# One more 512 KB transfer in a load queue: sample 0 loaded a second time, into a slot that is still empty

## The chip, the core and the metric

The kernel runs on one core of one Trainium2 chip. The core has a matrix engine (TensorE, "PE" in the profile), a vector engine (VectorE, "DVE"), three further engines that are used here for issuing and waiting alone (ScalarE "ACT", GpSimd "POOL", SyncE "SP"), and 16 DMA engines that move data between the memory outside the core (HBM, "DRAM" in the code) and its own memory (SBUF, 128 partitions). The metric is the time of one execution in microseconds (us). The kernel before takes 323.55 us, the median of three runs (323.35, 323.55 and 323.56).

## The reference

There are 128 samples, each a matrix x[b] of 128 channels by 1024 points in 32-bit floats (512 KB). Each sample has a subject number between 0 and 7, which chooses one of eight 128 by 128 weight matrices:

```
w = weights[subjects]                       # 128 x (128, 128)
out = x + einsum('bct,bcd->bdt', x, w)      # out[b] = x[b] + w[b]^T x[b]
```

So 64 MB (67.1 million bytes) are read, as many are written, and each sample needs one 128 by 128 by 1024 product and one addition.

## The kernel before

**Tiles and slots.** The samples go in turns of four (`G * H` = 2 * 2), so there are `NT` = 32 turns. SBUF holds `x_all`, which is cut into `SLOTS` = 12 slots; a slot has room for the four samples of a turn, 16 KB in each of the 128 partitions. Turn i uses slot i % 12. The result is added into the slot in place and is stored from there, so a slot is free for the next load when its store has landed.

**Loads (ACT's queue).** ScalarE issues 128 transfers, one for each sample, in order (lines 206 to 210). `load` writes a sample as 128 partitions by 4 KB, and reads it as 32 pieces of 16 KB, which is what the rearrangement with `ROWS` = 4 says: one piece in DRAM is four rows of the sample, which go to four partitions. From turn 12 on, ScalarE waits ahead of the four loads of a turn until the store of the turn that had this slot has landed. The semaphore of a slot, `s_slot[k]`, is raised by 16 for each of the four loads and for the store. Sample 0 and 1 raise `s_head`, so that the first product can start early.

**Products (PE).** Per half turn (two samples), TensorE waits for `s_go` (the weights stand ready) and `s_ready` (the data has landed; GpSimd turns the landing of loads into it, lines 212 to 217), and does four products of 128 by 128 by 512 into a half of PSUM.

**Additions (DVE).** Per half turn, VectorE waits for the products and adds them to the slot in one operation of 128 by 2048 (line 180), then copies the weights of two samples of the next turn into their place (line 159).

**Stores (SP's queue).** SyncE waits for additions (`s_added`) and issues the stores. For the first 20 turns there is one store of 2 MB per turn, which waits for the additions of its own turn and of four more (`BEHIND`); the last 12 turns go in pairs (4 MB each). In a store of one turn each partition is read in one run of 16 KB and written to DRAM in four pieces of 4 KB. The last store is issued outside of the first critical block, behind waits that the end of the program needs.

**Order.** Nothing plans this order but the program itself: each engine runs its own list, and ACT's and SP's transfers are worked off by the same 16 DMA engines, each queue in its order.

Of the kernel before, what the change touches and what calls it, by code (L numbers as in the profile page):

```python
# [30 lines left out]
G = 2  # L31
H = 2
# [3 lines left out]
SLOTS = 12  # L36
# [9 lines left out]
DMA = 16  # L46
# [3 lines left out]
ROWS = 4  # L50
# [5 lines left out]
def transfer(nc, engine, out, in_):  # L56

    later, nc._always_lower_symbolic_ap = nc._always_lower_symbolic_ap, False  # L60
    ins, outs = engine.lower_ap_dma(in_), engine.lower_ap_dma(out)
    nc._always_lower_symbolic_ap = later
    return engine.add_instruction(
        mybir.InstDMACopy(
            name=nc.get_next_instruction_name(),
            engine=engine.engine,
            ins=ins,
            outs=outs,
            mode="Copy",
            cce_op=ALU.bypass,  # L70
            queue=QUEUES[engine.engine],
        )
    )


@with_exitstack
def kernel(
    ctx: ExitStack,
    tc: tile.TileContext,
    x: bass.AP,  # L80
    subjects: bass.AP,
    weights: bass.AP,
    out: bass.AP,
):
    nc = tc.nc
    B, C, T = x.shape
    S, _, D = weights.shape
    NT = B // (G * H)

    def sbuf(name, *shape, dtype=F32):  # L90
        return ctx.enter_context(nc.sbuf_tensor(name, list(shape), dtype)).ap()


    room = -(nc.sbuf_base + -nc.sbuf_base % 32) % ALIGN
    if room:
        sbuf("room", C, room // 4)
    x_all = sbuf("x_all", C, SLOTS * H * G * T)
    xs = [
        x_all[:, i * H * G * T : (i + 1) * H * G * T].rearrange("c (q t) -> c q t", t=T)
        for i in range(SLOTS)  # L100
    ]
    w_all = sbuf("w_all", C, S, D)
    ws = [sbuf(f"w{i}", C, 1, D) for i in range(H * G)]
    zeros = sbuf("zeros", C, N)
    given, near, wrap = (sbuf(name, 1, B, dtype=I32) for name in ("given", "near", "wrap"))
    index = sbuf("index", 1, B + H * G, dtype=I32)
    ps = [
        ctx.enter_context(nc.psum_tensor(f"ps{i}", [D, G, T], F32)).ap() for i in range(P_SLOTS)
    ]

    s_given = tc.alloc_semaphore("s_given")
    s_wall = tc.alloc_semaphore("s_wall")
    s_index = tc.alloc_semaphore("s_index")
    s_zeros = tc.alloc_semaphore("s_zeros")
    s_product = tc.alloc_semaphore("s_product")
    s_added = tc.alloc_semaphore("s_added")

    s_ready = tc.alloc_semaphore("s_ready")
    s_go = tc.alloc_semaphore("s_go")

    s_slot = [tc.alloc_semaphore(f"s_slot{k}") for k in range(SLOTS)]
    s_head = tc.alloc_semaphore("s_head")

    def emptied(i):
        turns = i // SLOTS
        return DMA * (H * G + 1) * turns - (DMA * G if i >= SLOTS and i % SLOTS == 0 else 0)

    def load(engine, i, q):
        transfer(
            nc,  # L130
            engine,
            xs[i % SLOTS][:, q, :],
            x[i * H * G + q].rearrange("(a r) t -> a (r t)", r=ROWS),
        ).then_inc(s_head if i * H * G + q < G else s_slot[i % SLOTS], DMA)

    def store(i, n):
        at = i % SLOTS * H * G * T
        return transfer(
            nc,
            nc.sync,  # L140
            out[i * H * G : (i + n) * H * G].rearrange("g d t -> d g t"),
            x_all[:, at : at + n * H * G * T].rearrange(
                "d (o t) -> d o t", o=1 if i >= NT - WHOLE else n
            ),
        )

    def subjects_of(i):
        _, subject = nc.values_load_multi_w_load_instructions(
            index[0:1, i] if isinstance(i, slice) else index[0:1, bass.ds(i * (H * G), H * G)],
            engines=[mybir.EngineType.DVE],  # L150
            min_val=0,
            max_val=S - 1,
            skip_runtime_bounds_check_because="the index is clamped on the chip above",
        )
        return subject

    def place(h, subject):
        for q in range(h * G, (h + 1) * G):
            copy = nc.vector.tensor_copy(ws[q], w_all[:, bass.ds(subject[q], 1), :])  # L159
        copy.then_inc(s_go, 1)  # L160

    def multiply(slot, h):
        nc.tensor.wait_ge(s_go, 1).then_inc(s_go, -1)
        nc.tensor.wait_ge(s_ready, 1).then_inc(s_ready, -1)  # L164
        for q in range(h * G, (h + 1) * G):
            for t in range(0, T, N):
                at = slot * (H * G * T) + (q * T + t)
                mm = nc.tensor.matmul(  # L168
                    ps[h][:, q % G, t : t + N],
                    ws[q][:, 0, :],  # L170
                    x_all[:, bass.ds(at, N)],
                    start=True,
                    stop=True,
                )
        mm.then_inc(s_product, 1)

    def add(slot, h):
        mine = x_all[:, bass.ds(slot * (H * G * T) + h * G * T, G * T)]
        nc.vector.wait_ge(s_product, 1).then_inc(s_product, -1)  # L179
        nc.vector.tensor_tensor(  # L180
            mine, ps[h].rearrange("d g t -> d (g t)"), mine, ALU.add
        ).then_inc(s_added, 1)

    with tc.tile_critical():  # L184

        nc.sync.dma_start(given, subjects.rearrange("(o b) -> o b", o=1)).then_inc(s_given, DMA)
        nc.sync.dma_start(w_all, weights.rearrange("s c d -> c s d")).then_inc(s_wall, DMA)

        nc.vector.memset(zeros, 0.0).then_inc(s_zeros, 1)  # L189
        nc.tensor.wait_ge(s_zeros, 1)  # L190
        for _ in range(IDLE):
            nc.tensor.matmul(  # L192
                ps[P_SLOTS - 1][:, G - 1, :N], zeros[:, :D], zeros, start=True, stop=True
            )

        nc.vector.memset(index[:, B:], 0).then_inc(s_index, 1)  # L199
        nc.vector.wait_ge(s_given, DMA)  # L200
        nc.vector.tensor_scalar(near, given, -S, S - 1, ALU.max, ALU.min).then_inc(s_index, 1)  # L201
        nc.vector.wait_ge(s_index, 2)
        nc.vector.tensor_scalar(wrap, near, 0, S, ALU.is_lt, ALU.mult).then_inc(s_index, 1)  # L203
        nc.vector.wait_ge(s_index, 3)
        nc.vector.tensor_tensor(index[:, :B], near, wrap, ALU.add).then_inc(s_index, 1)  # L205
        for i in range(NT):
            if i >= SLOTS:
                nc.scalar.wait_ge(s_slot[i % SLOTS], emptied(i))
            for q in range(H * G):
                load(nc.scalar, i, q)  # L210

        for i in range(NT):
            if i == 0:
                nc.gpsimd.wait_ge(s_head, DMA * G).then_inc(s_ready, 1)
                nc.gpsimd.wait_ge(s_slot[0], DMA * G).then_inc(s_ready, 1)
            else:
                nc.gpsimd.wait_ge(s_slot[i % SLOTS], emptied(i) + DMA * H * G).then_inc(s_ready, H)

        for i in [*range(NT - SLOTS), *range(NT - SLOTS, NT, PAIR)]:
            n = 1 if i < NT - SLOTS else PAIR  # L220
            nc.sync.wait_ge(s_added, (i + n + (BEHIND if i < NT - LAST else 0)) * H)
            if i + n < NT:
                store(i, n).then_inc(s_slot[i % SLOTS], DMA)


        nc.vector.wait_ge(s_index, 4)
        nc.vector.wait_ge(s_wall, DMA)
        subject = subjects_of(slice(0, H * G))
        for h in range(H):
            place(h, subject)  # L230
        with nc.vector.Fori(0, NT) as turn:  # L231
            subject = subjects_of(turn + 1)
            for h in range(H):
                add(turn % SLOTS, h)
                place(h, subject)
        with nc.tensor.Fori(0, NT) as turn:
            for h in range(H):
                multiply(turn % SLOTS, h)

    with tc.tile_critical() as waits:  # L240
        for i in range(NT - SLOTS, NT - PAIR, PAIR):
            nc.scalar.wait_ge(s_slot[i % SLOTS], emptied(i + SLOTS))
    last = store(NT - PAIR, PAIR)

    tc.add_manual_dep(
        last.ins,
        waits.name,
        mybir.DependencyInfo(mybir.DependencyClass.NoSync, mybir.DependencyReason.SCHED_ONLY),
        reason="the end of the program waits for it",
    )  # L250
# [27 lines left out]
```

## Time and profile before

| what | value |
|---|---|
| time, median of three runs | 323.55 us (323.35 to 323.56) |
| profiled execution, span from the first to the last instruction | 322.2 us |
| PE busy | 246.3 us, 76% of the span |
| DVE busy | 165.7 us, 51% |
| bytes moved by DMA | 134.76 MB, 418 GB/s on average |

The profile is of one execution. The page gives its span and no other time of its own; the median is 1.35 us longer than that span, which is what lies around the first and last instruction (and the difference between one execution and another). Two parts of the page are used below beside the totals: the share of time in which the 16 DMA engines had a packet under way, in 40 equal slices of the span (about 8 us each, in tenths, 9 is 90% or more), and the DMA queues, of which q10 is the one that ScalarE issues on (its 67.12 MB are the loads) and q1 is that of SyncE (the stores and the weights).

### The profile page before, as it was taken

The page shows a single profiled execution, that of the slowest core. Times are in us where ns is not written, and L with a number is a line of the kernel's source. Part 1 is how long each engine was busy: PE and PEld are TensorE (multiplying, and loading weights), DVE is VectorE, ACT ScalarE, POOL GpSimd, SP SyncE. Part 2 cuts the span into 40 slices and gives each one's busy share as a digit, 9 for nine tenths or more (in the row PEclk, how much of TensorE's full clock was granted, in tenths as well). Part 3 has the DMA queues.
Part 4 walks back from the last instruction along what each step waited for, and adds up shares of the span by engine and source line. Part 5 has one row for each costly group of instructions (what it writes and reads, how often), then busy time and mean ns, then how long its engine had stood idle before and what let it go on. Part 6 is the DMA issues. An engine that isn't in the chain of part 4 may idle for free. (4 is left out here: it accounts for less than half of the span.)

```text
span 322.2 us, 2368 instructions
## 1 busy us (share of the span) xinstructions
PE 246.3 (76%) x518; PEld 101.8 (32%) x518; DVE 165.7 (51%) x202; POOL 0.2 (0%) x4
## 2 busy tenths in 40 slices
PE   6999999999996974975987489885699994972000
PEld 2344444444442421331333134332244431430000
DVE  2276776777677345354355344762657666254000
POOL 0000000000000000000000000000000000000000
PEclk9799999999999797797899899997999998698555
DMA  7999999999999999999999999999999999999996
GB/s 271 425 429 429 425 423 401 429 425 423 425 423 427 430 431 429 423 425 423 427 421 429 429 433 427 423 425 423 427 423 429 429 431 427 427 435 433 419 427 264
DMA packets 11315, 134.76 MB, mean 418 GB/s; under 512 B 2481, under 2 KB 3506, under 8 KB 3506
## 3 DMA queue, kind: packets, MB, share of 16 engines
q10 hardware_dynamic: 6144, 67.12, 49.6%
q1 hardware_dynamic: 5170, 67.64, 49.5%
q14 instruction: 1, 0.01, 0.0%
HBM read 67.63 MB, written 67.11 MB: 418 GB/s over the span
## 5 line engine op out<-in xcount | busy, mean ns | idle before, releaser
L168 PE MATMUL ps<-x_all,w 128*128 x512 | 241.3, 629 | 44.1 <-PEq L164 38.4
L180 DVE TENSOR_TENSOR x_all<-ps,x_all 128x2048 f32 x64 | 146.7, 2292 | 122.7 <-DVEq L179 122.7
L168 PEld LDWEIGHTS ps<-x_all,w 128*128 128x128 f32 x512 | 100.0, 201 | 185.7 <-issue 185.2
L159 DVE COPY w<-w_all 128x128 f32 x132 | 23.2, 219 | 4.7 <-DMA w_all<-in_L_cond_weights_dram 4.7
L192 PE MATMUL ps<-zeros 128*128 128x512 f32 x6 | 4.9, 988 | 1.7 <-DVE zeros L189 1.7
L192 PEld LDWEIGHTS ps<-zeros 128*128 128x128 f32 x6 | 1.8, 328 | 3.7 <-issue 2.1
L189 DVE MEMSET zeros<- 128x512 f32 x1 | 0.5, 485 | 1.0 <-SPq L184 1.0
L201 DVE TENSOR_SCALAR near<-given 1x128 int32<-1x128 int32 x1 | 0.2, 214 | 0.6 <-DMA given<-in_itok_B_dram 0.6
L205 DVE CUSTOM_DVE_ANT_0 index<-near,wrap 1x256 uint16<-1x256 uint16 x1 | 0.3, 280 | 0.0
L203 DVE TENSOR_SCALAR wrap<-near 1x128 int32<-1x128 int32 x1 | 0.2, 215 | 0.0
L265 POOL MEMSET const-bfloat16-1.0<- 128x1 bf16 x1 | 0.1, 102 | 0.0
L265 POOL MEMSET const-uint8-127<- 128x1 uint8 x1 | 0.1, 102 | 0.0
L265 POOL MEMSET const-float32-0.0<- 128x1 f32 x1 | 0.1, 99 | 0.2 <-issue 0.2
L265 POOL MEMSET const-float32-1.0<- 128x1 f32 x1 | 0.1, 99 | 0.0
L265 DVE BASE_LOAD x1 | 0.0, 21 | 0.1
L199 DVE MEMSET index<- 1x4 int32 x1 | 0.1, 62 | 0.0
## 6 DMA issues: line engine op xcount, KB each, us to landing
x_all<-in_x_dram ACTq DMA_DIRECT2D x128, 512.0 KB, 30.7
out_dram<-x_all SPq DMA_DIRECT2D x20, 2048.0 KB, 17.0
out_dram<-x_all SPq DMA_DIRECT2D x6, 4096.0 KB, 30.5
w_all<-in_L_cond_weights_dram SPq DMA_DIRECT2D x1, 512.0 KB, 5.5
given<-in_itok_B_dram SPq DMA_DIRECT2D x1, 0.5 KB
```

Source lines behind the costliest of these rows:

```text
L159: copy = nc.vector.tensor_copy(ws[q], w_all[:, bass.ds(subject[q], 1), :])
L168: mm = nc.tensor.matmul(ps[h][:, q % G, t : t + N], ws[q][:, 0, :], x_all[:, bass.ds(at, N)], start=True, stop=True,)
L180: nc.vector.tensor_tensor(mine, ps[h].rearrange("d g t -> d (g t)"), mine, ALU.add).then_inc(s_added, 1)
L189: nc.vector.memset(zeros, 0.0).then_inc(s_zeros, 1)
L192: nc.tensor.matmul(ps[P_SLOTS - 1][:, G - 1, :N], zeros[:, :D], zeros, start=True, stop=True)
L199: nc.vector.memset(index[:, B:], 0).then_inc(s_index, 1)
L201: nc.vector.tensor_scalar(near, given, -S, S - 1, ALU.max, ALU.min).then_inc(s_index, 1)
L203: nc.vector.tensor_scalar(wrap, near, 0, S, ALU.is_lt, ALU.mult).then_inc(s_index, 1)
L205: nc.vector.tensor_tensor(index[:, :B], near, wrap, ALU.add).then_inc(s_index, 1)
L265: nc = _bacc.Bacc("TRN2", target_bir_lowering=False, num_devices=1)
```

## The change

Behind the four loads of turn 5 (the sixth slot), ScalarE issues one more transfer. It reads sample 0 again, in the same 32 pieces of 16 KB as its first load did, and writes each piece whole into one partition: partitions 0, 4, 8, up to 124, at the place in `x_all` where slot 11 begins (the twelfth slot; four samples of 4 KB each fill it, so 16 KB is the slot's whole room in a partition). It raises a new semaphore, `s_twice`. Ahead of the loads of turn 11, which are the first to fill this slot, ScalarE waits until the transfer has landed. No engine reads what it wrote, and turn 11's loads write over it.

```diff
     s_slot = [tc.alloc_semaphore(f"s_slot{k}") for k in range(SLOTS)]
+    s_twice = tc.alloc_semaphore("s_twice")
     s_head = tc.alloc_semaphore("s_head")
...
+    def twice(engine):
+        at = (SLOTS - 1) * H * G * T
+        transfer(
+            nc,
+            engine,
+            x_all[::ROWS, at : at + ROWS * T],
+            x[0].rearrange("(a r) t -> a (r t)", r=ROWS),
+        ).then_inc(s_twice, DMA)
...
         for i in range(NT):
             if i >= SLOTS:
                 nc.scalar.wait_ge(s_slot[i % SLOTS], emptied(i))
+            if i == SLOTS - 1:
+                nc.scalar.wait_ge(s_twice, DMA)
             for q in range(H * G):
                 load(nc.scalar, i, q)
+            if i == 5:
+                twice(nc.scalar)
```

## The prediction

> **What bounds the kernel now.** I read the slices of the span first, then the DMA queues, then the waits, and last the stretches one by one. These are rows of the page:
>
> ```profile
> span 322.2 us, 2368 instructions
> PE 246.3 (76%) x518; PEld 101.8 (32%) x518; DVE 165.7 (51%) x202; POOL 0.2 (0%) x4
> ...
> DMA  7999999999999999999999999999999999999996
> ...
> q10 hardware_dynamic: 6144, 67.12, 49.6%
> q1 hardware_dynamic: 5170, 67.64, 49.5%
> ```
>
> No compute engine is near full, but the DMA row has a 9 in 38 of 40 slices, and the two queues' packets together took 99.1% of what 16 engines have in the span. PE and DVE wait for data; the DMA engines wait for nobody. That is an average, so it has to hold in each stretch. In this view of stretches the columns are the stretch and its length, the busy time of PE, PEld, DVE and POOL, the granted TensorE clock, the DMA share and GB/s:
>
> ```profile
> 0.00:8.00 8.00, 4.93 (x6) 1.85 (x6) 1.57 (x9) 0.20 (x4) 1.00 0.75 266
> 8.00:48.00 40.00, 39.24 (x85) 16.41 (x86) 25.28 (x31) 0.00 (x0) 0.96 1.01 427
> 48.00:56.00 8.00, 8.00 (x20) 3.33 (x18) 5.74 (x9) 0.00 (x0) 1.00 0.99 395
> 62.00:165.00 103.00, 85.19 (x179) 35.30 (x178) 57.08 (x69) 0.00 (x0) 0.92 1.01 426
> 232.00:246.00 14.00, 13.32 (x31) 5.87 (x32) 7.97 (x11) 0.00 (x0) 1.00 1.00 424
> 284.00:322.20 38.20, 7.13 (x16) 2.96 (x16) 7.12 (x9) 0.00 (x0) 0.66 0.93 396
> ```
>
> From 8 us on, the share is 0.99 to 1.01 in every stretch but the last, whatever is moved: loads alone (8 to 48), loads and stores together (62 to 165), and also from 232 to 246, where the stores had run dry. The queues of that last stretch:
>
> ```profile
> q10 hardware_dynamic: 526, 5.82, 98.2%
> q1 hardware_dynamic: 23, 0.11, 2.0%
> ```
>
> The loads that were queued filled the engines there by themselves. When one queue is empty the other covers, so the end is set by the sum of all bytes. The end of the program says the same. This is SyncE's view of its waits:
>
> ```profile
> SPq L274 <- DMA out_dram<-x_all: 25.5, 1, 25.5
> ```
>
> The last store (4 MB) is out for 25.5 us. Alone at 427 GB/s its 4.19 million bytes need 9.8 us; some 15.7 us of older stores stood ahead of it. So the last addition could come 15 us later without moving the end.
>
> **The change, part by part.**
>
> *The transfer itself.* It adds 512 KB, 524,288 bytes, to ACT's queue. Three rows price it. The loads: 49.6% of 322.2 us is 159.8 us for 67.12 MB, 2.381 us per MB, so 1.248 us for 0.5243 MB. The stores: 49.5% is 159.5 us for 67.64 MB, 2.358 us per MB, 1.236 us. The stretch from 8 to 48, loads alone at 427 GB/s: 1.228 us. The new transfer is not quite either form: it reads as a load does (16 KB runs of DRAM), but writes 16 KB into one partition where a load writes 4 KB into each of four. No row has that write. From below it is bounded by zero (in full cover), which the shares of 0.99 to 1.01 speak against: idle engines are found at the two ends alone (0.25 of the first 8 us, 0.07 of the last 38.2, which by the slices lies in the last 8), and the transfer is in neither. From above the nearest other 512 KB of unlike form is the weights, in pieces of 512 bytes:
>
> ```profile
> w_all<-in_L_cond_weights_dram SPq DMA_DIRECT2D x1, 512.0 KB, 5.5
> ```
>
> 5.5 us from issue to landing, beside the first loads; if the new transfer held all 16 engines so long, it would cost 5.5 us. I take 1.24 us, since both neighbours in form agree on it: the load has its reading side, and a store of 2 MB reads 16 KB out of a single partition at the same price, which shows that one partition can be emptied at an engine's full rate (that it can be filled so is the guess).
>
> [...]
>
> *Where it stands.* ACT's own issues before the change, cut at the place of the new one and at turn 11 (each row: least, median and longest issue in ns, first and last start; the last row of each cut is the time to landing):
>
> ```profile
> L63 ACTq DMA_DIRECT2D x_all<-in_x_dram x24: 532/618/1014, 0.9 to 16.0; - x24
> ...
> L63 ACTq DMA_DIRECT2D x_all<-in_x_dram x2: 891/1656/2422, 17.0 to 17.9; - x2
> DMA to landing us min/median/max: 19.5/19.6/19.8
> ...
> L63 ACTq DMA_DIRECT2D x_all<-in_x_dram x44: 532/701/2422, 0.9 to 41.1; - x44
> ...
> L63 ACTq DMA_DIRECT2D x_all<-in_x_dram x5: 1049/1050/1050, 41.1 to 45.5; - x5
> DMA to landing us min/median/max: 29.2/32.6/35.9
> ```
>
> 24 loads are issued by 17.0 us; the new transfer takes the place of the 25th, and should land some 19.5 us later, about 36.5 us. One issue more on ACT is about 1 us; ACT only issues and waits, and its queue is 19 us deep by then, so the issue hides behind that backlog. Without the backlog it would cost its microsecond.
>
> *The wait ahead of turn 11.* The 45th load is issued at 41.1 + 1.05, about 42.2 us, and later by about as much as the queue is longer. The transfer has landed 5.7 us before: the wait costs nothing. Behind it on ACT stand the loads of turns 11 to 31. Were it to bite, the loads already queued cover it: the last load ahead of it (issued at 41.1) lands 29.2 us later, so the wait would have to be that long before an engine ran empty.
>
> *What becomes late.* The loads of turns 6 to 11 land 1.24 us later. PE, DVE and SP do not notice in this part: by the row of additions below, eight half turns take 14.5 to 39.0, so 3.5 us each and 7.0 us a turn, while four loads take 4.9 us. Turn 6 starts its products at about 8.8 + 6 * 7.0 = 50.8 us, and its first load lands at 36.5.
>
> ```profile
> L168 PE MATMUL ps<-x_all,w x72: 592/592/1061, 8.8 to 41.8; 128*128 x72
> ...
> L180 DVE TENSOR_TENSOR x_all<-ps,x_all x8: 2292/2292/2293, 14.5 to 39.0; 128x2048 f32 x8
> ```
>
> So the first store is issued when it was before, at 48.4 us by SyncE's own list, whose row reads start, length, and what:
>
> ```profile
> 48.37 7.63 SPq L63 DMA_DIRECT2D out_dram<-x_all  x2
> ```
>
> From the handover on, loads and stores share the engines and each queue carries 1.24 us more backlog; the later additions come 1.24 us later, which the 15.7 us ahead of the last store hide, and the last store ends 1.24 us later because all bytes ahead of it do.
>
> *The rest.* One semaphore, one wait instruction: nothing on a path that ends last.
>
> *The sum.* On the profiled execution: 322.2 + 1.24 = 323.4 us of span. The median stands 1.35 us above that span, 323.55 + 1.24 = 324.79, say 324.8 us, 0.38% more.
>
> **The rivals.**
>
> *Filling one partition is slower than filling four.* If two pieces get in each other's way and go at half the rate, the price doubles: 2.48 us, 326.0 us. At the weights' 5.5 us it would be 329.1. For it: no row shows such a write. Against it: stores empty a single partition at full rate. [...]
>
> *It is given back at the handover (not slower).* From 48 to 56 us, where the first stores meet the loads, 395 GB/s were moved instead of 427: 8 * (1 - 395/427) = 0.60 us lost. With the loads shifted against the stores, this loss could vanish. Then 323.55 + 1.24 - 0.60 = 324.19 us. It decides at once: 0.59 us has to be returned for "within 0.2%" and 1.24 us would be needed for no change. Against it: the first store is still issued on a full load queue, so the two still meet.
>
> *It is hidden, or not carried out.* Were the end set by anything but bytes, 323.5 us would stay. Against it: no stretch has idle DMA engines, and the changed program has the transfer, between the 24th and the 25th load, as one copy of 32 by 4096.
>
> **How the numbers follow.** A change of 0.2% (0.65 us) is about what can be told from none; the three runs lie within 0.21 us. Forecast 0.78, its own range 324.4 to 325.2 (the price from 1.23 to 1.25, and the run's scatter and shifted alignment on both sides); slower filling 0.08 (326.0 and above); given back 0.07 (324.2); hidden 0.04 (323.5); and 0.03 for a faster run, for which I see no mechanism. The range 324.2 to 326.0 takes in the forecast, the given-back case and the lower half of the slow filling. Slower by over 0.2%: 0.78 + 0.08 and a little of the given-back case, 0.88; within 0.2%: 0.09; faster: 0.03.
>
> **What would show it.** In the changed profile: 0.52 MB more in q10 with a share of both queues still at 99%; the transfer landing near 36.5 us and the 45th load not held; the stretch 8 to 48 still at 427 GB/s (a slow filling shows as a dip near 35 us); the first store still near 48.4 us; the last store's end about 1.24 us later. The prediction is wrong if the dip is there, if the stretch 48 to 56 comes back to 427, or if the DMA share falls below 0.99 anywhere between 8 and 320 us.

## The result and the profile after

The changed kernel takes 324.38 us, the median of five runs (324.1 to 324.54), against 323.35 us of the kernel before on the same chip (five runs, 322.75 to 323.56): a ratio of 1.0033, with a 95% interval from 1.0022 to 1.0044. That is 1.03 us more, between 0.7 and 1.4. A second measurement with five runs of the changed and nine of the old kernel (e8_again among the experiments below) gave 324.46 against 323.22 us, 1.24 us more, ratio 1.0040 (1.0026 to 1.0053). So the change makes the kernel slower by some 1.0 to 1.25 us, 0.3 to 0.4%. One of the twelve runs of e11_weights below took 329.57 us, 5.1 us over the fastest of its kernel, and is left out as a slow one.

The page of the changed kernel: span, engines, the DMA engines' busy share and GB/s in 40 slices, and the two queues.

```profile
span 322.3 us, 2369 instructions
PE 251.0 (78%) x518; PEld 103.5 (32%) x518; DVE 165.7 (51%) x202; POOL 0.2 (0%) x4
...
DMA  7999999999999999999999999999999999999997
GB/s 281 425 425 427 425 423 411 427 429 425 423 423 429 428 427 427 429 427 425 423 429 425 427 431 425 429 425 423 425 429 425 427 431 427 427 425 429 451 411 309
...
q10 hardware_dynamic: 6192, 67.64, 49.9%
q1 hardware_dynamic: 5170, 67.64, 49.5%
```

q10 has 48 packets and 0.52 MB more, which is the new transfer: 32 pieces and 16 semaphore updates. Both queues together take 99.4% of 16 engines' span. The stretches, with the same columns and bounds as before the change:

```profile
0.00:8.00 8.00, 4.76 (x6) 1.86 (x7) 1.84 (x10) 0.20 (x4) 1.00 0.78 281
8.00:48.00 40.00, 39.79 (x91) 16.80 (x92) 26.00 (x31) 0.00 (x0) 1.00 1.01 426
48.00:56.00 8.00, 8.00 (x20) 3.42 (x19) 6.07 (x7) 0.00 (x0) 1.00 1.00 401
62.00:165.00 103.00, 85.53 (x176) 35.21 (x175) 56.00 (x66) 0.00 (x0) 0.92 1.01 426
232.00:246.00 14.00, 14.00 (x31) 5.79 (x30) 7.25 (x7) 0.00 (x0) 0.92 1.01 425
284.00:322.30 38.30, 8.83 (x16) 3.53 (x16) 7.00 (x9) 0.00 (x0) 0.65 0.95 405
```

The stretch with the new transfer (8 to 48) moves 426 GB/s, against 427 without it, and no stretch shown from 8 us on has idle engines (a share of 1.00 or 1.01) but the last (0.95). ACT's issue of the new transfer, the first row, with its time to landing, and the issues around the wait (the last load of turn 10 and the first three of turn 11):

```profile
L63 ACTq DMA_DIRECT2D x_all<-in_x_dram x1: 616/616/616, 16.6 to 16.6; - x1
DMA to landing us min/median/max: 19.3/19.3/19.3
...
L63 ACTq DMA_DIRECT2D x_all<-in_x_dram x4: 891/1044/2422, 41.1 to 44.2; - x4
```

It is issued at 16.6 us and has landed at 35.9 us; turn 11's first load follows the issue at 41.1 after 1.05 us, at 42.2 us, just as before. The transfer had landed 6.3 us before the wait could hold that load, so the wait cost nothing.

**Why the two spans shown differ by 0.1 us only.** The profile of before is one execution, and not a typical one. In all five runs of the changed kernel the time is 1.7 to 1.8 us over the span (324.1 with 322.3, 324.54 with 322.8), while before I took 1.35 us from a span of one execution and a median of others. It holds for the kernel before too: its nine runs in the second measurement took 322.95 to 323.41 us over spans of 321.2 to 321.6 us, again 1.7 to 1.8 us more. So the execution that was profiled there belongs to a time of about 324.0 us, some 0.5 to 0.7 us over its medians. Something that made it long can be seen at the end. These are the stretch of the body and the last 4 us, first of the kernel before, then of the changed one:

```profile
8.00:318.00 310.00, 241.34 (x512) 99.97 (x512) 164.15 (x195) 0.00 (x0) 0.91 1.01 427
318.00:322.00 4.00, 0.00 (x0) 0.00 (x0) 0.00 (x0) 0.00 (x0) 0.50 0.23 98
```

```profile
8.00:318.00 310.00, 246.24 (x512) 101.66 (x512) 163.81 (x192) 0.00 (x0) 0.90 1.01 427
318.00:322.00 4.00, 0.00 (x0) 0.00 (x0) 0.00 (x0) 0.00 (x0) 0.50 0.48 205
```

To 318 us both moved 427 GB/s. Then the old one had 98 GB/s * 4 us = 0.39 MB left to move and the new one 0.82 MB, and both ended at nearly the same time, since in the old one the 16 engines did not finish together: the 16 semaphore updates of the last store lie between 319.5 and 321.3 us (15 of them by 320.5), in the new one between 320.7 and 321.4. The data packets of the two queues add up to 317.86 us per engine before and 318.94 after, so the work grew by 1.08 us; the end went by the engine that was last. Two single profiles can hide a change of 1 us in this way, and the medians of runs don't.

### The profile page after: what moved, and what is told of

It reads as the page before. It is cut to its first block, busy times and chain, and to the rows that moved or that the text cites. A ratio compares the mean times of both kernels' runs of the same rounds, so it can differ in the third digit from the quotient of the medians.

```text
span 322.3 us, 2369 instructions
## 1 busy us (share of the span) xinstructions
PE 251.0 (78%) x518; PEld 103.5 (32%) x518; DVE 165.7 (51%) x202; POOL 0.2 (0%) x4
## 5 line engine op out<-in xcount | busy, mean ns | idle before, releaser
L178 PE MATMUL ps<-x_all,w 128*128 x512 | 246.2, 639 | 41.2 <-PEq L174 32.7
L178 PEld LDWEIGHTS ps<-x_all,w 128*128 128x128 f32 x512 | 101.7, 204 | 185.8 <-issue 185.2
```

The lines of the kernel that those rows point to most:

```text
L178: mm = nc.tensor.matmul(ps[h][:, q % G, t : t + N], ws[q][:, 0, :], x_all[:, bass.ds(at, N)], start=True, stop=True,)
```

## The experiments

My theory was that the bytes add up: the DMA engines never idle between 8 and 320 us (a share of 1.00 over that stretch of the kernel before), so added bytes cost their engines' time, wherever they stand and whatever waits for them. The rivals were that filling one partition is dear, that place or wait has a price, and that some is given back where the first stores meet the loads.

| label | edit | change of the median, us | ratio and interval |
|---|---|---|---|
| e8_again | the change itself | +1.24 | 1.0040 (1.0026 to 1.0053) |
| e1_four_one | four such transfers | +4.81 | 1.0148 (1.0132 to 1.0163) |
| e2_four_plain | four as ordinary loads | +5.12 | 1.0150 (1.0135 to 1.0166) |
| e3_four_band | four, each into 32 neighbouring partitions | +10.04 | 1.0304 (1.0290 to 1.0319) |
| e4_skip | one load of the kernel before left out | -1.24 | 0.9962 (0.9949 to 0.9975) |
| e5_on_sp | the transfer on SyncE's queue | +1.19 | 1.0036 (1.0022 to 1.0050) |
| e6_late | the transfer behind the last load | +1.28 | 1.0043 (1.0030 to 1.0057) |
| e7_bites | the transfer right ahead of its wait | +1.29 | 1.0040 (1.0027 to 1.0054) |
| e9_band_one | the one transfer into partitions 0 to 31 | +2.72 | 1.0086 (1.0069 to 1.0103) |
| e10_pair_one | the one transfer into 0, 2, 4, to 62 | +2.29 | 1.0064 (1.0051 to 1.0077) |
| e11_weights | the weights in larger pieces, no other change | +1.59 | 1.0048 (1.0039 to 1.0057) |

All ratios are to the kernel before, from runs on the same chip. They are not the quotients of the two medians, so the last two columns can differ by up to 0.3 us.

### The price by size: four times, the other form, and one load less

```diff
             if i == SLOTS - 1:
-                nc.scalar.wait_ge(s_twice, DMA)
+                nc.scalar.wait_ge(s_twice, DMA * ROWS)
...
+        for k in range(ROWS):            # in twice()
+            # e1_four_one:   x_all[k::ROWS, at : at + ROWS * T]            <- x[k]
+            # e2_four_plain: x_all[:, at + k * T : at + (k + 1) * T]       <- x[k]
```

> Four transfers in the place of one: samples 0 to 3 again, the k-th into partitions k, k+4, k+8 and so on, 16 KB into one partition each. Byte sum (the DMA engines never idle, so added bytes cost their engines' time): 4 * 1.23 = +4.9 us on the kernel before, 328.3 us, with the last addition still hidden. Given back at the handover of 48 to 56 us (a gain of about 0.2 that comes once): the price per transfer rises from the 1.03 us measured with one to 1.17 or more, +4.7. A price per transfer that grows because the later loads come late: over +5.5.

> The same four samples at the same place in ACT's queue, in the form of an ordinary load (4 KB into each of 128 partitions). Byte sum: +4.9 us, the same as with one-partition pieces within 0.1 (eight pieces per engine at 616 ns instead of 611 ns are 0.04 us). If filling one partition were the dearer form, this kernel would be over 1 us faster than the one with one-partition pieces; if it were the cheaper one by more than the 611 to 616 ns that the trace shows, slower.

Four transfers cost 4.81 us (4.3 to 5.3), 1.20 us each, so a price that grows with the number, over +5.5, is excluded. A gain of 0.2 us that comes once is not: the +4.7 us that it would give and the +4.9 of the bytes alone both lie in the interval. In the form of ordinary loads they cost 5.12 us. The difference of 0.3 us is within the intervals (by the ratios it is under 0.1 us); its direction is that of the pieces' durations in the trace, 611 ns for 16 KB into one partition and 616 ns for 16 KB into four, which makes 0.04 us of it. Filling one partition was not dearer: 1.20 us each against 1.28. The DMA rows of e1 for the transfers' stretch, in the middle, and its neighbours:

```profile
8.00:34.00 26.00, 26.00 (x56) 10.83 (x56) 15.36 (x18) 0.00 (x0) 0.93 1.01 428
34.00:44.00 10.00, 10.00 (x25) 4.30 (x24) 7.24 (x7) 0.00 (x0) 1.00 1.00 426
44.00:56.00 12.00, 12.00 (x29) 4.95 (x28) 8.12 (x12) 0.00 (x0) 1.00 1.01 410
```

```diff
-            for q in range(H * G):
+            for q in range(1 if i == LESS else 0, H * G):     # LESS = 18
                 load(nc.scalar, i, q)
...                                                             # and 16 less in the waits of that slot
```

> The kernel before with one load less: the first sample of turn 18 isn't loaded, so that its output is that of what stood in the slot. Byte sum: -1.23 us, 322.1 us, since 512 KB less go through engines that are busy throughout. If loads in mid-program are hidden behind stores or computing: no change, within 0.3 us.

One load less gives back 1.24 us (0.8 to 1.6), so loads in the middle of the program are not hidden. The price had the same size in both directions (+1.24 and -1.24 us), and in the middle of the program (turn 18) as at its start (behind turn 5).

### Place and wait

```diff
-            if i == 5:
-                twice(nc.scalar)
...
+        # e5_on_sp: twice(nc.sync), right behind the load of the weights
+        # e6_late:  behind the last load: wait_ge(s_slot[8], emptied(32)), twice(nc.scalar) into slot 8;
+        #           the program's end waits for s_twice
+        # e7_bites: if i == SLOTS - 1: twice(nc.scalar), then wait_ge(s_twice, DMA)
```

> The one extra transfer moved to SyncE's queue, behind the weights, where nothing else stands until the first store at 48 us; ACT's list keeps the wait ahead of turn 11. Byte sum: +1.0 to +1.25 us as in ACT's queue, since both queues share the 16 engines, though the first loads and so the first product come later. If what counts is the place in ACT's queue (loads of turn 6 and on coming late): no change, within 0.3 us. If a late first product counts: more than +1.5 us.

> The one extra transfer moved to the end: behind the last load, after a wait for the store of turns 20 and 21, into the slot of turn 20. Stores alone are left then, with some 20 us of them queued. Byte sum: +1.0 to +1.25 us again. If the price came from loads that are pushed back, nothing is pushed back here: no change, within 0.3 us.

> The one extra transfer moved down to right ahead of the wait, behind turn 10, so that ScalarE really waits: from 42 us on for some 30 us, with turns 11 and on behind it. Byte sum: the loads already queued and the first stores keep the engines busy meanwhile, so +1.0 to +1.25 us, and ACT's next load is issued near 72 us instead of 42. If a wait on ACT's list has a price of its own: ACT's queue runs empty, the engines idle for some us when the stores can't fill them, and the time is more than 2 us over the kernel before.

> The changed kernel once more, as the measure for the three others on the same chip: byte sum +1.23 us, by the runs so far +1.03 (0.71 to 1.42).

All four lie within 0.1 us of each other: +1.19, +1.28, +1.29 and +1.24, each with an interval of some 0.4 us to both sides. In e6 no load stands behind the transfer (it is issued at 263 us, after the last of them), so the price does not come from loads pushed back. In e7 the wait really holds ScalarE. Its issues of the transfer and what stands around it, then of what comes after the wait:

```profile
L63 ACTq DMA_DIRECT2D x_all<-in_x_dram x3: 1049/1049/1050, 39.4 to 41.6; - x3
DMA to landing us min/median/max: 13.5/15.4/33.7
...
L63 ACTq DMA_DIRECT2D x_all<-in_x_dram x3: 485/1203/1345, 75.3 to 77.0; - x3
```

ACT's transfer goes out at 41.6 us and its next load at 75.3 us (72 was expected), where the kernel before issued turn 11's first load at 42.2. The DMA engines stayed as busy (a share of 1.01 in both kernels). This is the stretch of that wait, first of e7, then of the kernel before:

```profile
43.00:73.00 30.00, 30.00 (x69) 12.42 (x68) 21.42 (x27) 0.00 (x0) 1.00 1.01 421
```

```profile
43.00:73.00 30.00, 30.00 (x69) 12.57 (x68) 22.23 (x25) 0.00 (x0) 1.00 1.01 422
```

A hold of 33 us on the engine that issues all loads cost nothing that can be told from the bytes (+1.29 us, against +1.24 in e8): the loads issued before were still being worked off (the transfer itself landed only 33.7 us after its issue), and the stores began meanwhile.

### Which partitions

The change writes into every fourth partition, which may have avoided what the prediction's rival feared, pieces in each other's way. So the same bytes went elsewhere:

```diff
-            x_all[::ROWS, at : at + ROWS * T],
+            # e3_four_band:  x_all[k * 32 : (k + 1) * 32, at : at + ROWS * T], k = 0 to 3
+            # e9_band_one:   x_all[: C // ROWS, at : at + ROWS * T]
+            # e10_pair_one:  x_all[: C // 2 : 2, at : at + ROWS * T]
```

> The same four transfers with one-partition pieces, but each into 32 neighbouring partitions (0 to 31, 32 to 63, 64 to 95, 96 to 127) instead of every fourth. Byte sum alone: +4.9 us, as with every fourth. Pieces that get in each other's way: the engines' pieces are longer than 611 ns, up to twice, and the price is up to 2 * 4.9 = +9.8 us. [...]

> The changed kernel with its one transfer written into partitions 0 to 31 instead of every fourth one, same bytes, same pieces, same place. If neighbouring partitions halve the rate, as four such transfers showed (+10.0 us, 2.5 us each, pieces of 1278 ns): +2.5 us, 325.7 us. If the four slowed each other and not themselves: +1.24 us.

> The same into every second partition, 0 to 62. If what counts is that pieces lie in neighbouring partitions: +1.24 us, or in between. If what counts is which half of the 128 partitions they reach (the even ones up to 62 reach none of the upper half): +2.5 us as with 0 to 31. [...]

Four transfers into neighbouring partitions cost 10.04 us, over twice the 4.81 us of every fourth. The stretches of e3 that answer to those of e1 above:

```profile
8.00:34.00 26.00, 25.80 (x59) 10.93 (x60) 16.04 (x19) 0.00 (x0) 1.00 1.02 428
34.00:44.00 10.00, 10.00 (x24) 4.01 (x23) 7.26 (x10) 0.00 (x0) 1.00 1.00 216
44.00:56.00 12.00, 12.00 (x29) 5.22 (x28) 8.90 (x10) 0.00 (x0) 1.00 0.99 419
```

From 34 to 44 us the engines are as busy as ever (1.00) and move 216 GB/s instead of 426: the pieces take about 1278 ns each (the median from 35 to 41 us) instead of 611. The bytes and their place in DRAM are those of e1, so the partitions alone make the difference. A busy share of 1.00 did not mean here that the engines ran at 426 GB/s. One transfer shows the same. The stretch with the transfer, first of e9 (0 to 31), then of e10 (every second to 62), then of e8, the change itself:

```profile
34.00:39.00 5.00, 5.00 (x13) 2.10 (x12) 4.19 (x4) 0.00 (x0) 1.00 0.98 252
```

```profile
34.00:39.00 5.00, 5.00 (x13) 2.10 (x12) 4.19 (x4) 0.00 (x0) 1.00 0.95 282
```

```profile
34.00:39.00 5.00, 5.00 (x13) 2.08 (x12) 4.19 (x6) 0.00 (x0) 1.00 1.00 423
```

In e10 no two of the partitions are neighbours, and yet the transfer costs 2.29 us (1.6 to 2.5), near the 2.72 us (2.2 to 3.3) of partitions 0 to 31. It did not take neighbouring partitions, then. What the slow transfers have in common is that each stays in one half of the partitions, 0 to 63 or 64 to 127, while the fast ones (611 ns a piece) go to both. In size, the 216 GB/s of e3 are half of the 426 of e1. Which engine served which piece is not seen in any run. Another thing that they have in common is left: in the slow transfers two or four pieces go to the same group of four partitions (0 to 3, 4 to 7, and so on, the groups that one piece of an ordinary load fills), in the change and in each transfer of e1 one piece does. No transfer that reaches both halves with two pieces to a group was run, so no run shows which of the two counts, or why.

### A version that might have been faster

In the trace the 1024 pieces of 512 bytes of the weights take 27.5 ns each, together 1.76 us of every engine, where a load of the same size takes 1.23 us. So, in the kernel before:

```diff
-        nc.sync.dma_start(w_all, weights.rearrange("s c d -> c s d")).then_inc(s_wall, DMA)
+        for k in range(S):
+            transfer(
+                nc, nc.sync, w_all[:, k, :], weights[k].rearrange("(a r) d -> a (r d)", r=8)
+            ).then_inc(s_wall, DMA)
...
-        nc.vector.wait_ge(s_wall, DMA)
+        nc.vector.wait_ge(s_wall, DMA * S)
```

> The kernel before, with the weights loaded by eight transfers, one for each subject, that read DRAM in 16 pieces of 4 KB instead of by one transfer in 1024 pieces of 512 bytes. Byte sum with the piece's form counted: the 1024 pieces take 27.5 ns each, 1.76 us of each engine; as 4 KB reads at the loads' rate 1.23 us, so -0.5 us, 322.7 us. If the write into 512-byte rows sets the pace, whatever the read: no change, within 0.2 us. If eight issues on SyncE (0.4 us each) delay the first product and that counts: slower.

It is slower by 1.6 us (1.3 to 1.8), where 0.5 us less was expected. The page shows where part of it is lost:

```profile
GB/s 236 395 426 426 422 430 422 424 432 428 426 424 428 422 425 432 426 426 424 428 422 428 432 426 428 422 428 422 428 430 426 426 426 428 422 442 434 426 430 256
...
w_all<-in_L_cond_weights_dram SPq DMA_DIRECT2D x8, 64.0 KB, 7.4
```

The first two slices move 236 and 395 GB/s, where the kernel before moved 271 and 425: 65 GB/s less over slices of 8 us are 0.5 MB, 1.2 us of the engines. The weights took a little less of the engines (128 pieces of 200 ns on average, 1.6 us of each engine instead of 1.76), but the loads beside them became dearer (693 ns at the median in the first 12 us instead of 611). The weights also came later: VectorE waited 12.7 us for them instead of 4.7, and the first product started at 16.6 us instead of 8.8. The last store was still out for 17.7 us, more than the 9.8 us of its own bytes, so nothing shows that this delay reached the end, but it was not tried alone. Why the transfers slow each other was not tried further. The page shows one more thing: no later slice but the last of this kernel falls under 422, so the dip where the first stores meet the loads (401 GB/s in that slice of the kernel before, 411 in the changed one) is not there, and the kernel is slower all the same.

## Why the prediction was right, point by point

- *The bound.* Right, and shown from both sides: 512 KB more cost 1.24 us (0.8 to 1.7) and 512 KB less give back 1.24 us (0.8 to 1.6), at the rate that the stretches show.
- *The price, 1.24 us.* Right: 1.03 and 1.24 us were measured for one and 1.20 us each for four. The packets' own sum grew by 1.08 us in the profile shown. The first time alone would not have decided it: 324.38 us lies just under the forecast's own range of 324.4 to 325.2 and nearer to the 324.19 of the given-back rival than to 324.8. Part of that is the kernel before, whose median over five runs was 323.35 and not the 323.55 of the first three; from there the same sum gives 324.59. What speaks for the full price is the change itself, +1.03 (0.7 to 1.4) and +1.24 (0.8 to 1.7), both above the rival's +0.64.
- *Filling one partition at the full rate.* The guess held (611 ns a piece), but the reason I gave was too short. That stores empty one partition at the full rate says nothing of which partitions the transfer spans; with 0 to 31 the transfer cost about twice as much (2.72 us against 1.24). The rival was real: its 2.48 us is about what 0 to 31 and 0 to 62 cost (2.72 and 2.29). That pieces in each other's way go at half the rate was my estimate, taken from no row; the change's own pieces took 611 ns, and those of e3 about 1278. That the change is free of it was luck as far as the prediction goes: it did not ask what a transfer in one half would do.
- *Place, landing, wait.* Landing was expected near 36.5 us and came at 35.9. The wait was free, and in e7 it was free even where it held ScalarE for 33 us (+1.29 us, against +1.24 in e8). One detail was wrong: I expected the load behind the wait to be issued later because of a longer queue, and it was issued at 42.2 us as before. ACT's issues take 1.05 us each instead of 0.62 from about 17 us on, so something holds them back there, but the new transfer, although as large as a load, did not make them later; what they are held back by was not tried. And 36.5 us, given as the landing of turn 6's first load too, is right for the new transfer alone; that load landed at about 37.1 us, still some 13 us ahead of its products.
- *The compute side.* The first store went out at 46.2 us instead of 48.4, not at the same time: the first product started at 8.0 us instead of 8.8, and PE's granted clock was 1.00 from 8 to 48, against 0.96. Neither is seen to have moved the end.

```profile
46.18 0.65 SPq L63 DMA_DIRECT2D out_dram<-x_all  x1
...
SPq L288 <- DMA out_dram<-x_all: 23.8, 1, 23.8
```

- *The last store* waits 23.8 us, of which 9.8 us are its own bytes. Some 14 us of older stores stand ahead of it, so the cover of the last addition is still there. Its end was forecast 1.24 us later and is 0.1 us later in the two profiles shown (321.4 and 321.3 us), since the profile of before was a long one.
- *Given back at the handover.* It was not: 395 GB/s before, 401 and 381 in the two profiles of the changed kernel, so this loss scatters from run to run by itself. That it can vanish, e11 showed (426 GB/s from 48 to 56).
- *What lies around the span* was mis-sized: 1.35 us in the prediction, 1.7 to 1.8 us by runs that have both. The forecast of the time did not hang on it, but the span of 323.4 us did: 322.3 was profiled, 322.7 in e8. From the median of before, 323.35 - 1.8 + 1.24 = 322.8 us would have been forecast.
- *A sign of being wrong* was drawn too tightly: by single microseconds the DMA share does fall below 0.99 ahead of 320 us, to 0.69 from 318 to 319 in the changed kernel and to 0.08 from 319 to 320 in the kernel before. Over all of 8 to 320 us it is 1.01 and 1.00, and no idle stretch came with the change.

## What to carry to other kernels

Where the DMA engines were busy in every stretch, a transfer like the ones already there cost its bytes at the engines' rate (1.24 us for 512 KB, at 426 GB/s), and place and queue (+1.19 to +1.29 us) and a wait of 33 us (+1.29) added nothing that could be told, as long as something was queued; look at the busy share by stretch before pricing a wait. Read GB/s beside the busy share: in e3 the engines were busy 100% at half the rate (216 GB/s against 426), with transfers that each landed in partitions of one half. For a transfer that uses 32 of 128 partitions, try them spread over all 128, as 0, 4, 8, up to 124: 611 ns a piece here, against 1278 in 32 neighbouring ones.

## What the runs showed of the hardware that was not expected

- 32 pieces of 16 KB into 32 neighbouring partitions took about twice the time (e3: 216 GB/s over 10 us, 1278 ns a piece) that they took into 0, 4, 8, to 124 (e1: 426 GB/s, 611 ns), with a busy share of 1.00 in both. Into 0, 2, 4, to 62 they were slow too (e10: +2.29 us instead of +1.24, 282 GB/s from 34 to 39 us instead of 423).
- The 16 engines did not finish together, and the end went by the last of them: in the profile of before, their last updates were 1.8 us apart, in that of the changed kernel 0.7 us.
- Weights read in pieces of 4 KB instead of 512 bytes took a little less of the engines themselves (1.6 instead of 1.76 us) and yet made the program 1.6 us slower, with the loads beside them at 693 ns instead of 611.
